# A two-layer graph attention network on one core: graph 0's means written over the gathered sums, graph 14's row made by TensorE, a root moved behind two sums on GpSimd

## The chip, the cores and the metric

The kernel runs on one NeuronCore of a Trainium2 chip. A core has five engines with a queue each: TensorE (PE in the profile, with PEld for its weight loads), VectorE (DVE), ScalarE (ACT), GpSimd (POOL) and SyncE (SP), which here issues DMAs alone. Each works off its queue in order and waits on semaphores of the others. The metric is the device time of one execution in microseconds (us); lower is better. The time before is the median of three runs.

## The reference

x holds 16 graphs of 1024 nodes with 256 features; adj is one 1024 x 1024 mask, the same for all graphs. All is in float32. Cut to what matters:

```python
def _gat(inp, adj_mask, W, a):             # layer 0, slope 0.2; h is normed, then relu
    h = inp @ W
    f1, f2 = h @ a[:F, 0], h @ a[F:, 0]
    e = leaky_relu(f1[:, :, None] + f2[:, None, :], ALPHA)
    if adj_mask is not None:
        e = where(adj_mask > 0, e, NEG_INF)
    return elu(softmax(e, axis=2) @ h)

# layer 0
h = maximum(layernorm(x), 0)
res = relu(h @ mlp1_w + mlp1_b)                         # 256 -> 512
out = elu(_gat(res, None, W_fc, a_fc)) + res            # dense attention, 512
res = relu(out @ mlp2_w + mlp2_b)                       # 512 -> 256
out = elu(_gat(res, adj, W_hand, a_hand)) + res         # masked attention
x = x + relu(out)
# layer 1
h = maximum(layernorm(x), 0)
x = x + relu(softmax(masked leaky_relu scores, slope 0.01) @ (h @ W))
```

## The kernel before, in words

Nodes are tiled by 128 (NT = 8 tiles, two halves of TH = 4). Every graph b goes through these stages:

- first norm (`Norm`, norm1): statistics of each tile on VectorE (L262, L263), the root 1/sqrt(var + eps) of a half on GpSimd (`root`, L267 and L268), centring on VectorE (`center`, L272), transposes on TensorE (`turn`, L282) and their eviction on ScalarE (L286);
- `mlp1` (L456, L459) into resT, `Dense.project` (L470, evicted at L472, the query column moved by GpSimd at L474 and L475) into h_nat;
- the dense attention without its 1024 x 1024 products: rows are ranked by their score (`rank`, VectorE), scattered to DRAM in that order by GpSimd's indirect DMAs (`scatter`, L530), read back by SP (`read_sorted`, L574), summed from both ends (`sum_before`, `sum_behind`, L602 to L617), the running sums written as a fine table (L609) and a coarse one (`carry`, L621 to L631). `sign` (ScalarE, L553) counts for each node where its own score falls, `count` turns the counts into indices, and `gather` (GpSimd, L642) fetches for each node the fine sums and adds the coarse ones to them in `got`. `share` (L654 to L657) gives the denominators, `mean` (L664 on ScalarE, L666 on VectorE) the weighted means `hp`;
- `merge` transposes hp on TensorE (L713), takes the lower part (L715), two exponentials on ScalarE (L716, L717); `merge_end` adds on VectorE (L723) and GpSimd adds into resT (L724); `mlp2` follows (L731, L734);
- masked attention `Gnn0` ("a"): `project` (L322, L324), `vectors`, `row` (the query weights as a row on all partitions), `scale` (L369), `weight` (VectorE, L375), `product` (L385), `finish`, `combine` with the sums on GpSimd (L413, L414) and `update` of x on VectorE (L418);
- second norm (norm2), then masked attention `Gnn1` ("b") and the store.

`row` exists in two ways. For b in AHEAD (1 to 14) `send` transposes the column on TensorE (L243), copies it on ScalarE (L245), writes it to DRAM (L246), and `row(True)` reads it back to all partitions by a DMA on SP (L360). For the others eight transposes on TensorE write it to PSUM (L238), and ScalarE copies it in two pieces (L365).

Graph 0 is an exception (`split`): its first half of the dense attention is done by real products (`Dense.weight` L687, `Dense.product` L695, `product_mean` L702 to L706, into tiles hpd of the same tag `hp`), its second half by gathers as above.

The order of everything is written by hand. `at(lo, hi, steps)` puts steps into a table with due times in us; the table is sorted by these times and the steps are issued in that order (L1091), which is the order in each engine's queue. The times mean nothing else. GpSimd's instructions, too, are chained in this order. The stages of neighbouring graphs overlap; a graph comes every PERIOD = 142. For graph b's masked attention t0 is its base and lo = t0 + 18 for b in AHEAD.

Tiles come from pools by tag with a number of buffers: `hp` has 4, `part` 2, `e2` 3, `hm` 2, `att` 8; in PSUM `mm` 4, `tr` 2, `bc` 1. A tile waits until the earlier user of its buffer is read out.

The lines that the change touches, besides those in its diff: `first_norm` places norm1's statistics and roots; `masked_first` places `send`, `row`, `scale`, `weight`, `product`, `finish`, `combine`, `update`, `stats` and the two roots of norm2; the schedule of the opening is written out from START = -168. `early_gathers` places a middle graph's sixteen gathers: four fine ones at t0 + 41.5 and 42.5, four from t0 + 48.5, the coarse ones from t0 + 53.5.

Of the kernel before, what the change touches and what calls it, by code (L numbers as in the profile page):

```python
# [8 lines left out]
F32 = mybir.dt.float32  # L9
# [8 lines left out]
P = 128  # L18
# [13 lines left out]
def fast_path(ctx: ExitStack, tc: tile.TileContext, alarm, x, adj, w1, b1, w2, b2, w_fc, a_fc,  # L32
# [24 lines left out]
    NT = N // P  # L57
# [3 lines left out]
    TH = HALF // P  # L61
    R = H + 2
    K = H + 1
# [3 lines left out]
    work = ctx.enter_context(tc.tile_pool(name="work", bufs=2))  # L67
# [154 lines left out]
    def at(lo, hi, steps):  # L222
        for i, step in enumerate(steps):
            table.append((lo + (hi - lo) * i / len(steps), len(table), step))
# [212 lines left out]
    class Dense:  # L437
# [221 lines left out]
        def mean(self, h, u):  # L659
            n = TH // len(self.got[h])  # L660
            got, den = self.got[h][u // n][:, u % n, :], self.dens[h]
            name = f"{self.b}_{h}_{u}"
            part = work.tile([P, K], F32, tag="part", name=f"part_{name}")
            nc.scalar.activation(part, got[:, :K], AF.Copy, scale=den[:, 1, u:u + 1])  # L664
            hp = self.hps[h, u] = work.tile([P, K], F32, tag="hp", name=f"hp_{name}", bufs=TH)
            nc.vector.scalar_tensor_tensor(hp, got[:, K:], den[:, 0, u:u + 1], part,  # L666
                                           op0=OP.mult, op1=OP.add)

# [104 lines left out]
    def each(f, *ranges):  # L773
        out = [()]
        for r in ranges:
            out = [o + (i,) for o in out for i in r]
        return [partial(f, *o) for o in out]

    def first_norm(t0, b):

        n = norm1[b]
        lo = t0 - (62 if b == 2 else 33.5)
        at(lo, lo + 1, n.stats_steps(0))
        at(t0 - 13, t0 - 9, n.stats_steps(1))
        n.turn_at(t0 - (14.5 if b == 2 else 22), 0, 4 if b == 2 else 7)
        n.turn_at(t0 + 0.2, 1, 4)
# [49 lines left out]
    def gathers(d, h, lo, hi):  # L836
        at(lo, lo + 4, each(d.gather, [h], [0], range(TH)))
        at(hi, hi + 7, each(d.gather, [h], [1], range(TH)))
# [20 lines left out]
    def merges(lo, d, h):  # L859
        at(lo, lo + 9.2, each(d.merge, [h], range(HC)))  # L860
        at(lo + 2.5, lo + 11.7, each(d.merge_end, [h], range(HC)))

    def second_mlp(t0, b, after=0):
        d, m = dense[b], gnn0[b]
        for i, lo in enumerate((102.5, 104.8, 113, 116.5)):
            lo += t0 - 3.4 * last(b)
            at(lo, lo, [partial(d.mlp2, i // FC, i % FC)])
        t0 += after
        at(t0 + 135, t0 + 142, each(m.project, range(NT)))
        at(t0 + 141.9, t0 + 141.9, [m.extremes])  # L870

    def weights(m, t, n, lo, hi):
        at(lo, hi, each(m.weight, [t], [n], range(NT)))

    def masked_first(t0, b):
        m, n = gnn0[b], norm2[b]
        at(t0 + 1, t0 + 1, [m.vectors])
        lo = t0 + 11
        if b in AHEAD:
            at(t0 + 3.4, t0 + 3.4, [m.send])  # L880
            at(t0 + 6, t0 + 6, [partial(m.row, True)])
            lo += 7
        else:
            at(t0 + 4, t0 + 4, [m.row])
        at(t0 + 4.5, lo - 1, each(m.scale, range(NT)))
        weights(m, 0, 2, lo - 5.5, lo - 1)
        at(t0 + 10, t0 + 10, [partial(load_again, b)])
        if last(b, 2):
            for q, start in enumerate((0.5, 2, 4.2, 5.5)):
                at(t0 + start, t0 + start, [partial(dense[b].natural, q)])  # L890
        else:
            at(t0 + 4.5, t0 + 11, each(dense[b].natural, range(NT // 2)))
        pairs = [(t, 2) for t in range(0, NT, 2)]
        if last(b):
            pairs[-1:] = [(NT - 2, 1), (NT - 1, 1)]
        for t, n_t in pairs:
            start = lo + 3.5 * t
            at(start, start + 3.5 * n_t, each(m.product, [t], [n_t], range(NT)))
            if t:
                weights(m, t, n_t, start - 5.5, start + 1)  # L900
        for t in range(NT):
            end = lo + 7.2 + 7 * (t // 2) + 0.6 * (t % 2)
            if last(b) and t == NT - 2:
                end -= 3.5
            at(end, end, [partial(m.finish, t)])
            at(end + 1.2, end + 1.2, [lambda t=t: m.combine(t, dense[b].o_nat)])
            if last(b) and t >= NT - 2:
                at(end + 2.6, end + 2.6, [lambda t=t: m.add(t, dense[b].o_nat, nc.vector)])
                end -= 2
            at(end + 5.2, end + 5.2, [lambda t=t: m.update(t, xs[b])])  # L910
            end += 5.6 if last(b) else 6.2 if b == 0 else 9
            at(end, end, [partial(n.stats, t)])
        at(lo + 25 - 3.4 * last(b), lo + 25 - 3.4 * last(b), [partial(n.root, 0)])
        lo += 33.1 if last(b) else 35.5 if b == 0 else 38.5
        at(lo, lo, [partial(n.root, 1)])

    def last(b, n=1):
        return b >= NB - n
# [58 lines left out]
    AHEAD = range(1, NB - 1)  # L977
# [4 lines left out]
    START = -168.0  # L982
    n, d = norm1[0], dense[0]
# [7 lines left out]
    n = norm1[1]  # L991
# [26 lines left out]
    for t in range(TH):  # L1018
        lo = START + 95 + 7.1 * t
        at(lo, lo + 7, each(d.product, [t], range(NT)))  # L1020
        at(lo + 8.2, lo + 8.2, [partial(d.product_mean, t)])
    at(START + 100, START + 107, each(d.weight, [1], range(NT)))
    gathers(d, 1, START + 108, START + 114)
    e = dense[1]
    at(START + 95.5, START + 95.5, [e.columns])
    at(START + 98.5, START + 98.5, [e.row, e.highest])
    at(START + 99, START + 118, each(e.rank, range(NT)))
    at(START + 118, START + 118, [less_columns])
    merges(START + 125, d, 0)
    at(START + 135, START + 135, [partial(d.share, 1)])  # L1030
    at(START + 135.5, START + 137, each(d.mean, [1], range(TH)))
    merges(START + 138.2, d, 1)
    second_mlp(START + 39, 0, -13)
    at(START + 123.4, START + 141, each(e.project, range(NT), [0]))
    scatters(e, START + 126, START + 142)
# [1 line left out]
    at(START + 142.5, START + 142.5, [e.read_sorted])  # L1037
    at(START + 76, START + 76, [partial(load_first, 2)])
    first_norm(0, 2)
    at(START + 147, START + 147, [e.sums_begin])  # L1040
    at(START + 144, START + 158, each(e.sign, range(NT)))
    for h in range(2):
        at(START + 150 + 3 * h, START + 150 + 3 * h, [partial(e.sums_weights, h)])
        at(START + 151 + 5 * h, START + 156 + 5 * h, each(e.sum_before, tiles(h)))
# [6 lines left out]
    for b in range(NB):  # L1051
        base, after_base = base_of(b), base_of(b + 1)
        masked_first(base, b)
        second_norm(base, b)
        pairs = range(0, NT, 2)
# [25 lines left out]
        if b + 3 < NB:  # L1081
            lo = after_base - PERIOD + 86
            at(lo, lo, [partial(load_first, b + 3)])
            first_norm(after_base, b + 3)
# [5 lines left out]
    with tc.manual_schedule(engines={engine.PE, engine.DVE, engine.Activation, engine.SP}):  # L1090
        for _, _, step in sorted(table, key=lambda entry: entry[:2]):  # L1091
            traced = nc.cur_bb.bb.instructions
            n = len(traced)
# [424 lines left out]
def two_layer_gat(tc, *args):  # L1518
    nc = tc.nc
    with tc.tile_pool(name="alarm", bufs=1) as pool:  # L1520
        alarm = pool.tile([1, 1], I32, name="alarm")
        fast_path(tc, alarm, *args)
        with tc.If(nc.values_load(alarm[0:1, 0:1], min_val=0, max_val=1,
                                  skip_runtime_bounds_check_because="it is 0 or 1") > 0):
            general_path(tc, *args)
# [24 lines left out]
```

## Time and profile before

| what | us |
|---|---|
| three runs | 2348.07, 2344.05, 2342.45 |
| median | 2344.05 |
| the profiled execution, its own time | 2359.75 |
| its span, first to last instruction | 2357.9 |
| idle before GpSimd's norm roots (L267), until VectorE's statistics | 148.4 in 35 waits |
| VectorE idle before the update of x (L418), until GpSimd's sum | 55.5 in 14 waits |
| GpSimd idle before a fine gather, until the fine table landed | 41.9 in 7 waits |

The span is the time between the first and the last instruction in the profile; the profiled execution is some 16 us longer than the median of the runs. Idle time of an engine costs only where the engine that bounds the kernel waits for it. In a timeline line the columns are start, duration, engine, line, operation, output<-inputs, shape and count; the bracket gives the idle time before it and what ended that. Neighbouring records of one line are merged. [...]

### The profile page before, as it was taken

The page shows a single profiled execution, that of the slowest core. Times are in us where ns is not written, and L with a number is a line of the kernel's source. Part 1 is how long each engine was busy: PE and PEld are TensorE (multiplying, and loading weights), DVE is VectorE, ACT ScalarE, POOL GpSimd, SP SyncE. Part 2 cuts the span into 40 slices and gives each one's busy share as a digit, 9 for nine tenths or more (in the row PEclk, how much of TensorE's full clock was granted, in tenths as well). Part 3 has the DMA queues.
Part 4 walks back from the last instruction along what each step waited for, and adds up shares of the span by engine and source line. Part 5 has one row for each costly group of instructions (what it writes and reads, how often), then busy time and mean ns, then how long its engine had stood idle before and what let it go on. Part 6 is the DMA issues. An engine that isn't in the chain of part 4 may idle for free. (4 is left out here: it accounts for less than half of the span.)

```text
span 2357.9 us, 30868 instructions
## 1 busy us (share of the span) xinstructions
PE 2268.6 (96%) x9955; PEld 1747.4 (74%) x9955; DVE 1625.7 (69%) x4535; ACT 1241.3 (53%) x2744; POOL 951.4 (40%) x1212
## 2 busy tenths in 40 slices
PE   8989999999999999999999999999999999999888
PEld 6667787777878778786776877777786876877666
DVE  6666685866858567685866867576685856767655
ACT  5345655647365463745546374554736546373442
POOL 1153435354443536334263543526444353533420
PEclk9999999999999999999999999999999999999999
DMA  4658366572656747366573745657265673737500
GB/s 173 165 159 210 72 176 165 167 193 97 200 118 175 180 143 184 97 187 161 172 187 113 186 115 165 174 161 181 91 195 143 174 184 125 185 95 182 140 21 27
DMA packets 150874, 355.81 MB, mean 151 GB/s; under 512 B 11224, under 2 KB 62760, under 8 KB 146608
## 3 DMA queue, kind: packets, MB, share of 16 engines
q1 hardware_dynamic: 104080, 189.58, 28.8%
q0 software_dynamic: 45952, 163.99, 26.3%
q8 instruction: 82, 1.34, 0.2%
q14 instruction: 88, 0.72, 0.1%
q10 hardware_dynamic: 672, 0.17, 0.0%
HBM read 227.40 MB, written 126.30 MB: 150 GB/s over the span
## 5 line engine op out<-in xcount | busy, mean ns | idle before, releaser
L385 PE MATMUL ob<-hmb,attb 128*128 128x257 f32 x2048 | 467.9, 386 | 21.4 <-DVE attb L375 17.0
L470 PE MATMUL h<-wfc_sb,resT 128*128 128x257 f32 x2048 | 465.7, 380 | 0.0
L385 PE MATMUL oa<-hma,atta 128*128 128x258 f32 x2048 | 454.7, 381 | 7.2 <-DVE atta L375 7.1
L385 PEld LDWEIGHTS ob<-hmb,attb 128*128 128x128 f32 x2048 | 387.2, 192 | 88.1 <-DVE attb L375 21.0
L385 PEld LDWEIGHTS oa<-hma,atta 128*128 128x128 f32 x2048 | 387.6, 190 | 67.0 <-issue 5.1
L470 PEld LDWEIGHTS h<-wfc_sb,resT 128*128 128x128 f32 x2048 | 379.5, 190 | 53.5 <-issue 0.7
L724 POOL TENSOR_TENSOR resT<-resT,e 128x512 f32<-128x512 f32 x128 | 163.6, 1278 | 371.4 <-DVE e L723 330.1
L375 DVE SCALAR_TENSOR_TENSOR atta<-rowsa,qwda,edge 128x256 f32<-128x256 f32 (+1 forms) x520 | 268.4, 545 | 27.6 <-PE oa L385 12.8
L413 POOL TENSOR_TENSOR posa<-posa,onat 128x256 f32<-128x256 f32 x118 | 98.7, 836 | 461.8 <-ACT posa L401 461.6
L375 DVE SCALAR_TENSOR_TENSOR attb<-rowsb,qwdb,edge 128x256 f32<-128x256 f32 (+1 forms) x536 | 247.9, 503 | 8.9 <-PE ob L385 5.5
L427 ACT ACTIVATE rb<-ob,recb 128x256 f32<-128x256 f32 x128 | 59.0, 475 | 346.1 <-DVE recb L425 329.4
L456 PE MATMUL m<-hT,w_sb 128*128 128x512 f32 x512 | 235.0, 598 | 0.5 <-ACT posa L401 0.5
L731 PE MATMUL m<-resT,w_sb 128*128 128x512 f32 x512 | 230.3, 596 | 4.3 <-POOL resT L724 4.3
L642 POOL DMA_INDIRECT got<-coarse,k x124 | 200.7, 1618 | 38.9 <-issue 37.7
L400 ACT ACTIVATE ea<-oa,reca 128x256 f32<-128x256 f32 x128 | 60.7, 474 | 271.2 <-DVE reca L397 262.1
L715 DVE TENSOR_SCALAR e<-hpT 128x512 f32<-128x512 f32 x128 | 88.3, 690 | 134.3 <-PE hpT L713 101.4
L731 PEld LDWEIGHTS m<-resT,w_sb 128*128 128x128 f32 x512 | 93.9, 191 | 106.3 <-issue 90.9
L456 PEld LDWEIGHTS m<-hT,w_sb 128*128 128x128 f32 x512 | 92.6, 193 | 95.9 <-issue 91.7
L642 POOL DMA_INDIRECT got<-fine,k x124 | 125.7, 1013 | 74.4 <-DMA fine<-xs 41.9
L530 POOL DMA_INDIRECT sorted<-hnat,place x128 | 131.9, 1030 | 39.6 <-issue 20.5
L553 ACT ACTIVATE junk<-r,fs 128x1024 int8<-128x1024 f32 x124 | 142.4, 1149 | 8.7 <-POOL fs L474 5.3
L716 ACT ACTIVATE e<-e 128x512 f32<-128x512 f32 x128 | 80.7, 631 | 84.2 <-DVE e L715 84.1
(186 smaller groups left out, 3445.8 us busy)
## 6 DMA issues: line engine op xcount, KB each, us to landing
xs<-sorted SPq DMA_DIRECT2D x32, 1028.0 KB
fine<-tt SPq DMA_DIRECT2D x32, 1026.0 KB
fine<-xs SPq DMA_DIRECT2D x32, 1026.0 KB
x<-in_x_dram SPq DMA_DIRECT2D x16, 1024.0 KB
xn<-in_x_dram SPq DMA_DIRECT2D x15, 1024.0 KB
out_dram<-x SPq DMA_DIRECT2D x28, 512.0 KB
coarse<-carry SPq DMA_DIRECT2D x32, 256.5 KB
r<-row_r SPq DMA_DIRECT2D x14, 512.0 KB
```

Source lines behind the costliest of these rows:

```text
L375: nc.vector.scalar_tensor_tensor(a_t[:, :n * P], self.rows[:, i], self.qwd[:, 1, j:j + 1], edge[:, j, i], op0=OP.max, op1=OP.mult)
L385: nc.tensor.matmul(self.out[t][:, :F + self.ONES], lhsT=self.att[t0, j][:, (t - t0) * P:(t - t0 + 1) * P], rhs=self.hm[:, j, 2:2 + F + sel ...
L413: adder.tensor_add(pos, pos, o_nat[:, t, :])
L456: nc.tensor.matmul(ps, lhsT=w1_sb[:, kc, c * P:(c + 1) * P], rhs=hT[:, kc, h * HALF:(h + 1) * HALF], start=(kc == 0), stop=(kc == FC - 1))
L470: nc.tensor.matmul(ps[:, :F + 1], lhsT=self.resT[:, kc, t * P:(t + 1) * P], rhs=wfc_sb[:, kc, g, :], start=(kc == 0), stop=(kc == HC - 1))
L530: made = nc.gpsimd.indirect_dma_start(out=sorted_d[self.b % 2], out_offset=bass.IndirectOffsetOnAxis(ap=self.place[:, t:t + 1], axis=0), i ...
L553: nc.scalar.activation(junk, self.r2, AF.Sign, bias=self.fs[:, 0, t:t + 1], accum_out=self.signs[:, t:t + 1])
L642: nc.gpsimd.indirect_dma_start(out=got[u // n][:, u % n, :], out_offset=None, in_=(coarse_d if coarse else fine_d)[self.b % 2][:, :], in_o ...
L715: nc.vector.tensor_scalar_min(e, ps, 0.0)
L716: nc.scalar.activation(e, e, AF.Exp)
L724: nc.gpsimd.tensor_add(dst, dst, e)
L731: nc.tensor.matmul(ps, lhsT=w2_sb[:, kc, c * P:(c + 1) * P], rhs=self.resT[:, kc, h * HALF:(h + 1) * HALF], start=(kc == 0), stop=(kc == H ...
```

## The change

Five things change.

1. `mean` writes graph 0's hp over the half of the gathered tile that it has just read, instead of into a tile of the tag `hp`.
2. The opening: the first half of graph 2's first statistics and root comes at due time -49 instead of -62; graph 0's gathers come 7 to 8 earlier; `product_mean` 0.6 earlier; `share`, `mean` and the merges of its second half 5, 5 and 2.2 earlier; graph 1's `sign` steps 14 to 8 earlier.
3. Graph 14's row in `Gnn0` is made by `row()` on TensorE and ScalarE, and no longer by `send` and `row(True)`. The later steps keep their places (lo is still t0 + 18).
4. The root of norm2's first half comes at lo + 31.5 instead of lo + 25 for graphs 1 to 14. On GpSimd it was between the fourth fine gather and the sums of tiles 6 and 7; it is now behind these sums and the fifth gather.
5. Graph 0 and the last graph keep their place for this root (lo + 25 and lo + 21.6).

```diff
             part = work.tile([P, K], F32, tag="part", name=f"part_{name}")
             nc.scalar.activation(part, got[:, :K], AF.Copy, scale=den[:, 1, u:u + 1])
-            hp = self.hps[h, u] = work.tile([P, K], F32, tag="hp", name=f"hp_{name}", bufs=TH)
+            hp = self.hps[h, u] = got[:, K:] if self.split else work.tile(
+                [P, K], F32, tag="hp", name=f"hp_{name}", bufs=TH)
             nc.vector.scalar_tensor_tensor(hp, got[:, K:], den[:, 0, u:u + 1], part,
                                            op0=OP.mult, op1=OP.add)
...
     def first_norm(t0, b):
         n = norm1[b]
-        lo = t0 - (62 if b == 2 else 33.5)
+        lo = t0 - (49 if b == 2 else 33.5)
         at(lo, lo + 1, n.stats_steps(0))
...
         lo = t0 + 11
         if b in AHEAD:
+            lo += 7
+        if b in AHEAD and not last(b, 2):
             at(t0 + 3.4, t0 + 3.4, [m.send])
             at(t0 + 6, t0 + 6, [partial(m.row, True)])
-            lo += 7
         else:
             at(t0 + 4, t0 + 4, [m.row])
...
-        at(lo + 25 - 3.4 * last(b), lo + 25 - 3.4 * last(b), [partial(n.root, 0)])
+        root = lo + (21.6 if last(b) else 25 if b == 0 else 31.5)
+        at(root, root, [partial(n.root, 0)])
...
         at(lo, lo + 7, each(d.product, [t], range(NT)))
-        at(lo + 8.2, lo + 8.2, [partial(d.product_mean, t)])
+        at(lo + 7.6, lo + 7.6, [partial(d.product_mean, t)])
     at(START + 100, START + 107, each(d.weight, [1], range(NT)))
-    gathers(d, 1, START + 108, START + 114)
+    gathers(d, 1, START + 101, START + 106)
...
     merges(START + 125, d, 0)
-    at(START + 135, START + 135, [partial(d.share, 1)])
-    at(START + 135.5, START + 137, each(d.mean, [1], range(TH)))
-    merges(START + 138.2, d, 1)
+    at(START + 130, START + 130, [partial(d.share, 1)])
+    at(START + 130.5, START + 135, each(d.mean, [1], range(TH)))
+    merges(START + 136, d, 1)
     second_mlp(START + 39, 0, -13)
     at(START + 123.4, START + 141, each(e.project, range(NT), [0]))
...
-    at(START + 144, START + 158, each(e.sign, range(NT)))
+    at(START + 130, START + 150, each(e.sign, range(NT)))
```

## The prediction

> **What bounds the kernel now.** I read the busy shares and the slices first, then the timeline of TensorE for each place that the diff names, then the other engines there.
>
> ```profile
> PE 2268.6 (96%) x9955; PEld 1747.4 (74%) x9955; DVE 1625.7 (69%) x4535; ACT 1241.3 (53%) x2744; POOL 951.4 (40%) x1212
> PE   8989999999999999999999999999999999999888
> ```
>
> TensorE (PE) is busy 96% of the span, so only its idle time can be won. The change adds and removes almost no matmuls (one transpose goes, eight come). Idle time lies in the first graphs and in the last, some 1 us a graph between. First place, graph 0's second merge (TensorE, except the third line, GpSimd's root of graph 2's first norm):
>
> ```profile
> 143.07 5.37 PE L470 MATMUL h<-wfc_sb,resT 128*128 128x257 f32 x24
> 152.65 0.33 PE L713 MATMUL hpT<-ident,hp 128*128 128x128 f32 x1 [1.73 <-DVE hp L666]
> 122.24 0.23 POOL L267 TENSOR_SCALAR rstd<-mv 128x4 f32<-128x4 f32 x1 [48.03 <-DVE mv L263]
> 124.80 2.01 PE L695 MATMUL od<-hnat,attd 128*128 128x257 f32 x8 [1.55 <-ACT hpd L705]
> 153.58 3.28 PE L470 MATMUL h<-wfc_sb,resT 128*128 128x257 f32 x8
> 167.91 1.13 PE L731 MATMUL m<-resT,w_sb 128*128 128x512 f32 x2 [1.14 <-POOL resT L724]
> 169.95 2.03 PE L731 MATMUL m<-resT,w_sb 128*128 128x512 f32 x2 [0.92 <-POOL resT L724]
> 176.90 7.14 PE L322 MATMUL pa<-wh_sb,oT 128*128 128x258 f32 x32
> ```
>
> PE runs out of projections at 148.4, waits for the means hp until 153.3, and later twice for the sums resT. GpSimd sat 48 us in front of a root; the gathers of graph 0 queue behind it and end near 137.
>
> Second place, a middle graph (GpSimd, VectorE, TensorE):
>
> ```profile
> 631.52 1.04 POOL L642 DMA_INDIRECT got<-fine,k  x1 [0.30 <-issue]
> 632.92 1.04 POOL L268 TENSOR_TENSOR rstd<-rstd,power 128x4 f32<-128x4 f32 x1
> 633.96 0.72 POOL L413 TENSOR_TENSOR posa<-posa,onat 128x256 f32<-128x256 f32 x1
> 635.51 0.93 DVE L418 SCALAR_TENSOR_TENSOR x<-ea,x 128x256 f32<-128x256 f32 x1 [2.97 <-POOL ea L414]
> 637.19 1.08 POOL L642 DMA_INDIRECT got<-fine,k  x1 [0.16 <-issue]
> 645.56 0.83 POOL L267 TENSOR_SCALAR rstd<-mv 128x4 f32<-128x4 f32 x1
> 648.32 1.43 PE L282 MATMUL nt<-ident,hn 128*128 128x128 f32 x8 [0.42 <-DVE hn L272]
> 780.27 4.55 PE L385 MATMUL ob<-hmb,attb 128*128 128x257 f32 x12 [3.55 <-DVE attb L375]
> ```
>
> VectorE waits 2.97 us for tile 6's sum, because GpSimd does four gathers and the root first. In this graph PE doesn't feel it; its one wait is for the second half's root. One graph later, where a table landed late, it does (3.55).
>
> Third place, graph 14:
>
> ```profile
> 2131.80 0.32 SPq L360 DMA_DIRECT2D rowsa<-row_a  x1
> 2136.31 0.48 DVE L375 SCALAR_TENSOR_TENSOR atta<-rowsa,qwda,edge 128x256 f32<-128x256 f32 x1 [3.02 <-DMA rowsa<-row_a]
> 2136.94 5.43 PE L385 MATMUL oa<-hma,atta 128*128 128x258 f32 x23 [2.44 <-DVE atta L375]
> ```
>
> The row's broadcast lands 4.5 us after its issue, and PE stands 2.44 us for it.
>
> [...] after the gap at 148.4 eight records take 3.28 us where 1.90 is usual. [...] the update at 635.51 takes 0.93 beside a GpSimd sum, 0.41 without one. [...] Here a row's way out and back is dearer: written at 2127.02, read issued at 2131.80, used at 2136.31.
>
> **Part 1, graph 0 and the opening: -4.9 us.** The eight gathers go ahead of the root. The tables they read are issued by 108.6 and eight gathers took 13.2 us (123.79 to 136.98), so they end some 10 us before their use at about 141. The four sums of statistics (0.54 us each, 2.2) leave the ranks on VectorE and come after them; so the mean of row tile 1 (VectorE 124.02) comes at 121.9, and the 1.55 wait goes: everything after is 1.55 earlier. The statistics then run 129.3 to 131.4 and meet nobody. The first merge's transposes end at 141.5.
> The share now follows the first merge's second sum, on VectorE at 140.8. On ScalarE the eight sign sums (1.27 each with their read-out) now stand between the steps of the merges; none is hidden by an idle queue here. In the order of the new due times: hnat copy to 141.8, sign to 143.2, two parts (0.65 each) to 144.5; VectorE's two means to 145.3, the held-back e(0,3) to 145.9; ScalarE's two exponentials 147.2, copy 147.5, sign 148.8, two parts 150.1; VectorE's last mean 150.85. It was 153.26. Writing into the gathered tile removes the wait for the first merge's four hp tiles, which otherwise would end at 141.5 anyway: worth nothing by itself. PE, having done h_5 at 145.0, transposes at 151.0, with h_6 and h_7 still ahead where only h_7 was: 153.58 against 151.0 + 1.74, a gain of 0.84. Then it runs beside ScalarE: h_6 at half clock to 154.1, hpT, h_7 to 156.3, hpT, m to 160.2, hpT, m to 164.1. ScalarE: copy 154.4, sign 155.6, e(1,1) 156.9, copy, sign 158.5, e(1,2) 159.8, bias 160.9, sign 162.3, e(1,3) 163.6. VectorE 164.3, GpSimd's sum 165.7 (was 169.9). The next m needs it at 166.7: the waits of 1.14 and 0.92 and the half clock after them go. Transposes 167.6 to 168.4, m to 171.9, and pa starts there, not at 176.90: 5.0 earlier. The following transposes need hn, which goes through xs, landing about 8.6 us after an issue near 161 (so long the second half took at 2124.93): 179.0 against 183.88, so 4.9. Graph 1's scatters move with the projections; its chain keeps its distance. Ends: -8 if the first gap keeps full clock and ScalarE is ahead[...].
>
> **Part 2, graph 14's row: -3.1 us.** Gone: one transpose, a copy (0.24), two DMAs, and on SP a wait in front of graph 14's x load and the first table write. New: eight transposes (0.87 on PE, as at 188.30) and two copies (1.07 on ScalarE, as at 189.37), in front of the o_nat copies; PE's ob products cover them but for some 0.25. ob then ends at 2134.75; the first weight follows the four sums before it on VectorE (end 2133.3) and is ready at 2133.8. So oa starts at 2134.75 instead of 2136.94: 2.2. Later in this graph GpSimd waited 3.67 for a table to land, then PE 3.43. With 0.5 MB less and SP free 6 us sooner that may shrink by 0 to 3.7; I take 0.9, since the queues thin out (DMA share 0.5) before it lands. Ends -1.5 and -6.
>
> **Part 3, the root in 14 graphs: +0.8 us.** The root (1.37 with its start) leaves the front of four sums and goes behind one gather. The sum of tile 6 ends 1.37 earlier, the update and two weights too. Then hn, next on VectorE, waits: sums end 635.66, gather to 636.9, root 1.40 to 1.63 (the later is the cost after a gather at 644.54), so hn at about 638.4; it was 638.04. VectorE trades a wait of 2.97 for 1.6 and 1.7. The third weight comes 0.3 to 0.5 later, and PE waits for it already (0.32 in most graphs). But the second root stands behind the same GpSimd work and isn't moved; PE's wait there (0.42 plus some 0.4 in its transposes) takes the delay up. Only graphs without that wait pay, two in this trace: 2 x 0.4. Ends: -7 (case C) and +15 (case D). The later root queues nothing else but three gathers, 1.4 later at the most.
>
> Sum: -4.9 - 3.1 + 0.8 = -7.2 us. The profiled execution took 2359.75 (span 2357.9), so 2352.5; the runs shown are 15.7 faster at the median, 2344.05, and I take the same difference: 2336.9.
>
> **Rivals.** A, this forecast: 0.46.
> B, ScalarE becomes the bound of the opening: six sign sums, 7.6 us, stand in front of the last exponential, and [...]GpSimd's last sum comes at 169 as before. For: ScalarE has more to do there than PE (about 20 us against 16). Against: the sum came out 4 us early. Left: about -2.2 from the row, 2342. 0.20.
> C, the update's gain reaches PE. For: six graphs show waits of 3.55, 3.43, 2.47, 1.61, 1.01 and 0.53 for the weight after tile 6's update; 1.37 less of each is 7.0. Against: the third weight ends last. 2329. 0.20.
> D, slower: the root behind the gather holds VectorE. With the gap of 0.31 after a gather and the root's longest durations (0.85 and 1.28) hn comes 1.1 us later, and if the second root slips as well, 14 x 1.1 = 15.4: 2351.5. It decides from 8.0 / 14 = 0.57 a graph. Against: the second root has the same work in front. 0.14.
>
> **How the numbers follow.** About 0.3% (7 us) is what a measurement can tell from no change. A lies on that edge: 0.26 of its 0.46 is faster, 0.20 same. B is same, C faster, D 0.12 slower and 0.02 same. Faster 0.46, same 0.42, slower 0.12. The range 2329 to 2348 leaves out D and the far half of C.
>
> **What would show it.** The gathers of graph 0 ahead of the root, the means' end near 151, pa near 172 and no wait for resT; in graph 14 oa without a wait for rowsa; in middle graphs tile 6's update waiting about 1.6, hn about 1.7, the transposes of the second half where they were. Wrong if pa starts after 175, or if the middle graphs' period changes by more than 0.5 us either way.

## The result, and the profile after

| | before | after |
|---|---|---|
| median of 20 runs, us | 2348.01 | 2352.30 |
| lowest to highest | 2340.48 to 2350.78 | 2346.50 to 2356.58 |
| ratio, 95% interval | | 1.0017 [1.0009, 1.0025] |
| profiled execution, its own time (span) | 2359.75 (2357.9) | 2353.19 (2351.5) |

The change makes the kernel slower by 0.17%, some 4 us; the forecast was 7.2 us faster. The two profiles say the opposite, 6.4 us less span. The profile of before is the odd one: its execution is 9 us above the slowest of the 20 timed runs. A second profile of before, taken later, has a span of 2350.0 us.

The first fence is TensorE's timeline in graph 0's second merge after the change, the second the same of graph 14. The change adds a line, so L666, L713 and L731 of before are L667, L714 and L732 here.

```profile
141.83 3.63 PE L470 MATMUL h<-wfc_sb,resT 128*128 128x257 f32 x16
150.77 0.44 PE L714 MATMUL hpT<-ident,got 128*128 128x128 f32 x1 [3.16 <-DVE got L667]
151.70 3.17 PE L470 MATMUL h<-wfc_sb,resT 128*128 128x257 f32 x8
161.19 7.03 PE L732 MATMUL m<-resT,w_sb 128*128 128x512 f32 x16
172.37 7.14 PE L322 MATMUL pa<-wh_sb,oT 128*128 128x258 f32 x32
```

```profile
2124.97 1.09 PE L238 MATMUL rowspsa<-ident,qwda 128*128 128x128 f32 x8 [0.37 <-ACT qwda L347]
2133.71 14.08 PE L385 MATMUL oa<-hma,atta 128*128 128x258 f32 x64
```

Both places are as forecast: the last mean is there at about 151, no line waits for resT, pa starts at 172.37 (176.90 before), and graph 14's oa follows without a wait for its row.

So the loss is to be looked for in the middle graphs. Here is the graph shown in the prediction, in the timelines of GpSimd, VectorE and TensorE after the change:

```profile
635.46 0.96 POOL L642 DMA_INDIRECT got<-fine,k  x1 [0.15 <-issue]
636.45 0.25 POOL L267 TENSOR_SCALAR rstd<-mv 128x4 f32<-128x4 f32 x1
638.02 1.21 POOL L642 DMA_INDIRECT got<-fine,k  x1 [0.19 <-issue]
639.53 1.33 POOL L642 DMA_INDIRECT got<-fine,k  x1 [0.31 <-issue]
641.17 0.94 POOL L642 DMA_INDIRECT got<-fine,k  x1 [0.30 <-issue]
645.37 0.86 POOL L267 TENSOR_SCALAR rstd<-mv 128x4 f32<-128x4 f32 x1
633.78 0.94 DVE L418 SCALAR_TENSOR_TENSOR x<-ea,x 128x256 f32<-128x256 f32 x1 [0.62 <-POOL ea L414]
637.86 0.73 DVE L272 TENSOR_SCALAR hn<-x,mv,rstd 128x256 f32<-128x256 f32 x2 [1.47 <-POOL rstd L268]
660.84 0.16 DVE L654 TENSOR_TENSOR den<-got,qd 128x4 f32<-128x4 f32 x1 [3.61 <-DMA got<-coarse,k]
648.16 1.41 PE L282 MATMUL nt<-ident,hn 128*128 128x128 f32 x8 [0.42 <-DVE hn L272]
663.88 0.33 PE L714 MATMUL hpT<-ident,hp 128*128 128x128 f32 x1 [0.24 <-DVE hp L667]
664.77 0.33 PE L714 MATMUL hpT<-ident,hp 128*128 128x128 f32 x1 [0.56 <-DVE hp L667]
665.43 0.33 PE L714 MATMUL hpT<-ident,hp 128*128 128x128 f32 x1 [0.33 <-DVE hp L667]
665.60 1.90 PE L470 MATMUL h<-wfc_sb,resT 128*128 128x257 f32 x8
```

And the lines of before, VectorE and TensorE, to which the forecast gave no place:

```profile
660.13 0.16 DVE L654 TENSOR_TENSOR den<-got,qd 128x4 f32<-128x4 f32 x1 [2.72 <-DMA got<-coarse,k]
664.71 0.33 PE L713 MATMUL hpT<-ident,hp 128*128 128x128 f32 x1 [0.34 <-DVE hp L666]
664.88 1.90 PE L470 MATMUL h<-wfc_sb,resT 128*128 128x257 f32 x8
```

The update's wait fell to 0.62, where 1.6 was forecast, and hn waits 1.47 (forecast 1.7). PE is at the second half's transposes (nt) 0.16 us earlier than before, yet at the projection behind the means (h, L470) 0.72 later. Between them PE waits for the means hp. These wait for VectorE's denominators (den), and those for the landing of the first half's coarse gathers.

To compare executions, times below are counted from a graph's first fine gather and averaged over 11 middle graphs (2 to 12). There the period, from one graph's first gather to the next's, is 140.44 us after the change and 138.93 with the root put back. Each is one execution: four more, whose middle graphs are those of before (before twice, the opening alone, the row alone), have periods of 139.08 to 140.55, so a period can be off by 1 us. The denominators are steadier: at 33.3 us after the change, at 32.3 to 32.6 in these four and with the root put back.

### The profile page after: what moved, and what is told of

It is laid out like the page before. It is cut to its first block, busy times and chain, and to the rows that moved or that the text cites. A ratio compares the mean times of both kernels' runs of the same rounds, so it can differ in the third digit from the quotient of the medians.

```text
span 2351.5 us, 30884 instructions
## 1 busy us (share of the span) xinstructions
PE 2266.0 (96%) x9962; PEld 1746.3 (74%) x9962; DVE 1639.0 (70%) x4535; ACT 1241.4 (53%) x2745; POOL 955.1 (41%) x1212
## 5 line engine op out<-in xcount | busy, mean ns | idle before, releaser
L385 PE MATMUL ob<-hmb,attb 128*128 128x257 f32 x2048 | 461.1, 382 | 18.7 <-DVE attb L375 14.8
L470 PE MATMUL h<-wfc_sb,resT 128*128 128x257 f32 x2048 | 465.7, 380 | 0.0
L470 PEld LDWEIGHTS h<-wfc_sb,resT 128*128 128x128 f32 x2048 | 379.4, 190 | 53.5 <-issue 0.7
L375 DVE SCALAR_TENSOR_TENSOR attb<-rowsb,qwdb,edge 128x256 f32<-128x256 f32 (+1 forms) x536 | 259.1, 525 | 8.9 <-PE ob L385 5.5
L732 PE MATMUL m<-resT,w_sb 128*128 128x512 f32 x512 | 229.6, 596 | 2.2 <-POOL resT L725 2.2
L732 PEld LDWEIGHTS m<-resT,w_sb 128*128 128x128 f32 x512 | 94.2, 192 | 104.6 <-issue 92.2
L530 POOL DMA_INDIRECT sorted<-hnat,place x128 | 132.2, 1033 | 39.6 <-issue 20.6
```

The source lines that it names most:

```text
L375: nc.vector.scalar_tensor_tensor(a_t[:, :n * P], self.rows[:, i], self.qwd[:, 1, j:j + 1], edge[:, j, i], op0=OP.max, op1=OP.mult)
L385: nc.tensor.matmul(self.out[t][:, :F + self.ONES], lhsT=self.att[t0, j][:, (t - t0) * P:(t - t0 + 1) * P], rhs=self.hm[:, j, 2:2 + F + sel ...
L470: nc.tensor.matmul(ps[:, :F + 1], lhsT=self.resT[:, kc, t * P:(t + 1) * P], rhs=wfc_sb[:, kc, g, :], start=(kc == 0), stop=(kc == HC - 1))
L530: made = nc.gpsimd.indirect_dma_start(out=sorted_d[self.b % 2], out_offset=bass.IndirectOffsetOnAxis(ap=self.place[:, t:t + 1], axis=0), i ...
L732: nc.tensor.matmul(ps, lhsT=w2_sb[:, kc, c * P:(c + 1) * P], rhs=self.resT[:, kc, h * HALF:(h + 1) * HALF], start=(kc == 0), stop=(kc == H ...
```

## The experiments

Each ratio is to runs of the kernel before taken next to those of the experiment. The medians of before in the four groups of experiments ran from 2341.5 to 2349.1 us, so only ratios are compared. What the profiles say of a kernel comes from one execution of it.

### One part at a time

Three theories. T1: the moved root costs its 0.8 us a graph or more and hides what the other parts gain. T2: the root is free, and the gains of the opening and of the row are lost later. T3: late tables alone, in some executions.

The root put back, all else as changed:

```diff
-        root = lo + (21.6 if last(b) else 25 if b == 0 else 31.5)
-        at(root, root, [partial(n.root, 0)])
+        at(lo + 25 - 3.4 * last(b), lo + 25 - 3.4 * last(b), [partial(n.root, 0)])
```

> The changed kernel with the root of the second norm's first half back at its old place (lo + 25), all else as changed. Theory T1, the moved root costs some 0.8 us in each of 14 graphs and hides what the other parts bring: this kernel is 6 to 9 us faster than the kernel before (ratio 0.996 to 0.9975), some 11 faster than the changed one; first fine gather to second root about 17.8 us again instead of 18.1. Theory T2, the opening's and the row's gains are lost further on and the root costs what the prediction said, 0.8 us in all: within 2 us of the changed kernel, ratio 1.001 to 1.003. Theory T3, the difference is how often a table lands late, whatever the root's place: ratio 0.999 to 1.003 with late landings as many as in the changed kernel.

The root alone moved, all else as before:

```diff
-        at(lo + 25 - 3.4 * last(b), lo + 25 - 3.4 * last(b), [partial(n.root, 0)])
+        root = lo + (21.6 if last(b) else 25 if b == 0 else 31.5)
+        at(root, root, [partial(n.root, 0)])
```

> The kernel before with the root alone moved to lo + 31.5. T1: 8 to 12 us slower than before, ratio 1.0035 to 1.005, the third weight after tile 6's update later in each graph and first gather to second root 0.27 us longer. T2: at most 1 us slower, ratio 1.000 to 1.0005. T3: anything from 1.000 to 1.003, by the late landings.

Only the opening with graph 0's means (the change's hunks for `mean`, `first_norm` and START):

```diff
-    gathers(d, 1, START + 108, START + 114)
+    gathers(d, 1, START + 101, START + 106)
...
-    at(START + 144, START + 158, each(e.sign, range(NT)))
+    at(START + 130, START + 150, each(e.sign, range(NT)))
```

> The kernel before with the opening alone (means over the gathered sums, gathers, merges, signs and graph 2's statistics at their new times); row and root as before. T1: graph 0's masked projection starts near 172.4 as in the changed kernel and the 4.5 us stay to the end, ratio 0.9975 to 0.9985. T2: the start is as early, but the end isn't, ratio 0.9995 to 1.002.

Only graph 14's row:

```diff
         if b in AHEAD:
+            lo += 7
+        if b in AHEAD and not last(b, 2):
```

> The kernel before with graph 14's row alone made by TensorE. T1 and T2 differ little here: the wait for the row goes (2.2 us), and what a late table costs in graph 14 may go too: ratio 0.997 to 0.9992. If the row's place doesn't matter since graph 14 waits for its table anyway, 0.9995 to 1.0005.

| run | ratio, 95% interval | worked out, us |
|---|---|---|
| root put back | 0.9966 [0.9954, 0.9978] | -8.0 |
| root alone | 1.0075 [1.0061, 1.0088] | +17.6 |
| opening alone | 0.9983 [0.9976, 0.9991] | -4.0 |
| row alone | 0.9988 [0.9979, 0.9997] | -2.8 |

The microseconds are the ratio less 1, times before's 2341.5. The opening and the row bring about what the forecast gave them, -4.9 and -3.1, and their sum is close to the gain with the root put back. The root loses 17.6 us alone, and 1.0017 / 0.9966 = 1.0051 or 12 us on top of the rest. T2 and T3 fall. T1 has the place, but for the root alone its range ended at 1.005: the loss is larger than it said.

### What of the moved root costs

T4: its place between the fifth and the sixth gather makes the later gathers land late. T5: VectorE is held, as hn waits for the root and the weights stand behind hn.

The changed kernel with the root in front of the fifth gather, still behind the sums:

```diff
-        root = lo + (21.6 if last(b) else 25 if b == 0 else 31.5)
+        root = lo + (21.6 if last(b) else 25 if b == 0 else 30.25)
```

> The whole change, but the first half's root comes directly behind the four sums of tiles 6 and 7 and in front of the fifth gather (in the changed kernel it is behind that gather). T4, the gathers: what costs is that the root now stands between the fifth and the sixth fine gather; in the traces so far the sixth to eighth start 0.3 us later, and the first half's coarse gathers land 1.0 us later (33.3 against 32.3 us after the first fine gather). With the root in front of the fifth gather these starts are as with the old place, the landing is back at 32.3, PE's wait for the means falls from 0.9 to about 0.4 us a graph, and the time is that of the kernel with the root put back: 0.9966 of before, 0.9955 to 0.9980. T5, VectorE: what costs is that hn waits for the root behind the sums, and the weights behind hn; the root still comes 3.1 us later than in the old place, so at least half of the cost stays: 0.999 to 1.001.

The root put back, and an addition of no use on GpSimd in front of the sixth gather:

```diff
+        def pause(self):
+            spare = small.tile([P, TH], F32, tag="spare", name=f"spare{self.name}")
+            nc.gpsimd.tensor_scalar_add(spare, self.mv[:, :TH, 1], EPS)
...
+        if b in AHEAD:
+            at(lo + 31.5, lo + 31.5, [n.pause])
```

> The change with the root put back in its old place, and in graphs 1 to 14 one small extra addition on GpSimd (128x4, some 0.3 us with its start, its result unused) between the fifth and the sixth fine gather. T4: 0.3 us there is the cost by itself: the landing of the first half's coarse gathers moves from 32.3 to about 33 us after the first gather, PE's wait for the means grows by 0.3 to 0.6 us a graph, 5 to 14 us in all: 0.999 to 1.002 of before. T5: VectorE isn't touched, so only the second root moves, by 0.3 us x 14 = 4 us at the most: 0.9966 to 0.9983.

The changed kernel, and then the kernel with the root put back, each with the load of a later x taken from among the gathers:

```diff
...
-            lo = after_base - PERIOD + 86
-            at(lo, lo, [partial(load_first, b + 3)])
+            lo = after_base - PERIOD + 94
+            at(lo, lo, [partial(load_first, b + 3, nc.scalar)])
```

> The whole change, and the load of the x of the graph after the next two (1 MB) is issued by ScalarE's queue behind the means, some 20 us later than SP issues it now (24.7 us after the first fine gather, in the middle of the coarse gathers); its first use is at 64 us. T4: the gathers land earlier without that megabyte among them[...]; PE's wait for the means (0.9 us a graph) is gone, and only the second root's 0.3 us stays: 0.9966 to 0.9985 of before. T5: PE's waits for the means are a by-product of its being late and VectorE is as before: 1.0005 to 1.002.

> The change with the root in its old place, and the same late load of x. T4: PE's wait for the means, 0.4 us a graph, goes: 5 us less than the kernel with the root put back, 0.9945 of before (0.993 to 0.9955). T5: nothing but a by-product, 0.9966 (0.996 to 0.9975).

Measured: 1.0055 [1.0035, 1.0076], 0.9983 [0.9973, 0.9993], 1.0015 [1.0005, 1.0025] and 0.9964 [0.9950, 0.9978]. Neither theory had the first number. With the root in front of the fifth gather, GpSimd and TensorE in the graph shown above:

```profile
635.48 1.07 POOL L268 TENSOR_TENSOR rstd<-rstd,power 128x4 f32<-128x4 f32 x1
636.75 1.21 POOL L642 DMA_INDIRECT got<-fine,k  x1 [0.19 <-issue]
638.26 1.33 POOL L642 DMA_INDIRECT got<-fine,k  x1 [0.31 <-issue]
639.90 0.94 POOL L642 DMA_INDIRECT got<-fine,k  x1 [0.31 <-issue]
647.92 1.41 PE L282 MATMUL nt<-ident,hn 128*128 128x128 f32 x8 [1.20 <-DVE hn L272]
```

A gather's issue takes 0.94 us at its quickest, but the two that follow this root take 1.21 and 1.33; after the change too it is the two behind the root, the sixth and seventh. The root sets VectorE's centring (hn) free. The first of the two issues runs beside it for most of its time (1.06 us on average after the change); the second meets only its last 0.17 us, and then other work of VectorE. In the old place the sixth issue has 0.69 us of centring beside it and takes 1.00, the seventh has none and takes 1.12. So these issues are longer in the new order, but what makes them so isn't shown. All four gathers go out late here (the last ends at 15.2 after the first gather, 14.6 with the old place); the second root starts 0.6 later, PE waits 1.20 for the transposes, and the denominators come at 33.9. Against T5, hn came earlier than in the old place (9.65 against 10.34), and PE's waits for the weights are few (1.6 us in the table below), and still the kernel is slower. T4 had wrongly assumed that equal work takes GpSimd equal time.

The pause leaves VectorE and the second root alone (17.85 against 17.83), moves the denominators from 32.3 to 32.8, and costs 4 us against the kernel with the root put back; the two intervals just overlap. It speaks for the landing, since T5's reason, a later second root, isn't there, but it doesn't decide: the ratio is below T4's range and at the upper end of T5's. The pause was no clean dose either: the seventh gather's issue became shorter by 0.15.

The late load changed nothing that can be told: both ratios lie in T5's ranges, and the fourth coarse gather lands at 33.1 as in the changed kernel. T4 was wrong to name this megabyte as what the gathers compete with.

### The landing, or the second root

T6: a graph pays for the landing of the fourth coarse gather. T7: it pays for the second root, for which PE waits 0.42.

The root of the first half in its old place, the second root one coarse gather earlier:

```diff
-        at(t0 + 53.5, t0 + 68, coarse)
+        at(t0 + 54.5, t0 + 68, coarse)
...
-        lo += 33.1 if last(b) else 35.5 if b == 0 else 38.5
+        lo += 33.1 if last(b) else 35.5 if b == 0 else 38.1
```

> The change with the first half's root in its old place, and in graphs 1 to 13 the root of the second half one coarse gather earlier on GpSimd (behind the first coarse gather instead of the second). T6, the landing: a graph's period follows the moment when the fourth coarse gather has landed (VectorE's denominators at 32.3, 32.8, 33.3 and 33.9 us after the first fine gather went with periods of 138.9, 139.7, 140.4 and 141.3). The second root, 1.9 us earlier, ends PE's wait of 0.42 us for the second half's transposes, but the wait for the means takes the same amount on; no gain: 0.996 to 0.9975 of before. T7, the second root: PE's wait for these transposes is what a graph pays, and 0.42 x 13 = 5.5 us go: 0.9943 (0.993 to 0.9955).

The first root behind all eight fine gathers, with the centring and transposes that need it moved:

```diff
+        root = lo + (21.6 if last(b) else 25 if b == 0 or last(b, 2) else 35.2)
+        at(root, root, [partial(n.root, 0)])
...
-            n.turn_at(t0 + 60.3, 0, 7)
+            n.turn_at(t0 + 64.3, 0, 4.2)
             n.turn_at(t0 + 67.3, 1)
```

> As the kernel with the root put back, but in graphs 1 to 13 the first half's root stands behind all eight fine gathers, and what needs it (the centring on VectorE, the transposes on PE) is moved behind the weights and some 3 us later in the products, so that neither engine has to wait for it. T6: the fifth to the eighth fine gather go out 1.4 us earlier than with the old place; the fourth coarse gather lands about 1 us earlier (31.3), PE's wait for the means goes (0.4 us a graph), 5 us in all: 0.9945 of before (0.993 to 0.9962). T7: the second root keeps its time, so no gain: 0.9966 (0.996 to 0.9985).

Both:

> The two moves of the last two runs together. T6 and T7 both: the landing is earlier and the second root too; PE loses the waits for the second half's transposes and for the means, 0.8 us a graph, 10 us in all: 0.992 of before (0.990 to 0.994). If it is no better than either alone, a further bound stands behind them (the next graph's tables).

Measured: 0.9986 [0.9979, 0.9993], 0.9927 [0.9914, 0.9940] and 1.0064 [1.0044, 1.0084]. The first ends PE's wait for the transposes and is slower than the kernel with the root put back: the second coarse gather goes out 1.3 us later, the denominators slip by 0.3, and PE, there earlier, waits 1.2 us for the means instead of 0.4. T7 falls, and T6 had not seen the later landing. The second is the fastest kernel of all, faster than both the kernel before and the changed one, and by more than T6 gave it (9 us against the root put back, not 5). PE hardly waits for the means; it waits more for the transposes' hn (12.3 us in the table below), and gains all the same. Its GpSimd, VectorE and TensorE:

```profile
628.47 0.96 POOL L642 DMA_INDIRECT got<-fine,k  x1 [0.15 <-PE ob L385]
632.22 0.94 POOL L642 DMA_INDIRECT got<-fine,k  x1 [0.31 <-issue]
633.19 0.36 POOL L267 TENSOR_SCALAR rstd<-mv 128x4 f32<-128x4 f32 x1
651.78 0.16 DVE L654 TENSOR_TENSOR den<-got,qd 128x4 f32<-128x4 f32 x1 [2.09 <-DMA got<-coarse,k]
655.82 0.87 PE L714 MATMUL hpT<-ident,hp 128*128 128x128 f32 x4
656.53 1.90 PE L470 MATMUL h<-wfc_sb,resT 128*128 128x257 f32 x8
```

The eighth gather goes out 11.9 us after the first (620.29), not 13.9 as after the change, and the last four issues take 0.94 to 0.96.

With both roots moved, the expected gain became the worst loss. TensorE:

```profile
659.14 0.33 PE L714 MATMUL hpT<-ident,hp 128*128 128x128 f32 x1 [0.27 <-DVE hp L667]
660.02 0.33 PE L714 MATMUL hpT<-ident,hp 128*128 128x128 f32 x1 [0.56 <-DVE hp L667]
660.69 0.34 PE L714 MATMUL hpT<-ident,hp 128*128 128x128 f32 x1 [0.34 <-DVE hp L667]
660.86 3.58 PE L470 MATMUL h<-wfc_sb,resT 128*128 128x257 f32 x8
```

PE comes earlier and the denominators come at 32.8 all the same, so it waits some 2.2 us a graph for the means. In 7 of 13 graphs the eight records of the projection behind that wait take 3.2 to 3.6 us instead of 1.90: there the wait is followed by 1.3 to 1.7 us of longer projection. In the graph of the fence the granted clock was 0.53 from 661.0 to 664.5. The size of the wait doesn't decide it: here it is 1.17 in three pieces, while another graph with 2.44 keeps 1.90.

### What makes the landing late

T9: the store of a finished graph, among the gathers, takes their place. T10: landings follow the issue alone. For the last winner also T8: the new order on PE and VectorE gained, not the gathers.

The root in its old place, only the centring and the transposes moved (the `turn_at` line above):

> A control to the kernel with the root behind the gathers: the root of the first half is in its old place, and only the centring on VectorE and the transposes on PE are moved, exactly as there. T6, the landing: the gathers go out when they did with the old place, the fourth coarse gather lands at 32.3 us after the first fine gather, and there is no gain: 0.9966 of before (0.9955 to 0.998). T8, the order on PE and VectorE is what gained (no wait of the third weight): 0.9927 (0.9914 to 0.994).

The changed kernel, and then the kernel with both roots moved, each with one late store by ScalarE's queue in place of two by SP:

```diff
...
+            elif t + n == NT and not last(b, 3):
+                late = base_of(b + 1) + 94
+                at(late, late, [lambda: m.store(0, NT, xs[b], b, nc.scalar)])
-            elif t % TH + n == TH:
+            elif t % TH + n == TH and last(b, 3):
                 at(end + 2.8, end + 2.8, [lambda t=t: m.store(t // TH * TH, TH, xs[b], b)])
```

> The whole change, and the two stores of a finished graph (512 KB each, issued by SP at 14 and 24 us after the first fine gather, among the gathers) become one of 1 MB, issued by ScalarE's queue some 48 us after it, for graphs 0 to 12. T9, the store collides: the late gathers lose their place to the store; without it the eighth fine gather lands by 20.5 us instead of 22.3, the fourth coarse by 31 instead of 33.2, PE's wait for the means (0.9 us a graph) goes: 0.995 to 0.998 of before. T10, the issue alone: landings follow the moment at which GpSimd issues the gathers, whatever else moves: as the changed kernel, 1.0017 (1.0005 to 1.0025).

> The kernel with both roots moved, and the same late store. T9: the coarse gathers land 1.5 to 2 us earlier (31.0 instead of 32.8), PE keeps neither the wait for the means nor that for the second half's transposes: 0.992 of before or less (0.988 to 0.994). T10: as with both roots moved, 1.0064 (1.004 to 1.0085).

The kernel before, once more:

> The kernel before, unchanged, for a second profile of it. If the profile of before was of an unusually long execution, this one's span is about 2345 us instead of 2357.9, with fewer gathers of GpSimd waiting for a table.

Measured: 0.9943 [0.9930, 0.9956], 0.9971 [0.9959, 0.9983] and 0.9939 [0.9921, 0.9956]; the second profile of before has a span of 2350.0 us (about 2345 was expected), with GpSimd waiting for a fine table in two of graphs 1 to 13 instead of five.

The late store takes the changed kernel from 1.0017 to 0.9971 and the one with both roots from 1.0064 to 0.9939, with no gather issued earlier by more than 0.1 us. Each of the next fences shows one instruction alone, the eighth fine gather of the graph shown above: first with the change, then with the late store.

```profile
L642 POOL DMA_INDIRECT got<-fine,k x1: 938/938/938, 641.2 to 641.2; - x1
DMA to landing us min/median/max: 8.7/8.7/8.7
```

```profile
L642 POOL DMA_INDIRECT got<-fine,k x1: 941/941/941, 638.7 to 638.7; - x1
DMA to landing us min/median/max: 6.5/6.5/6.5
```

Issued 13.9 us after the first gather in both, it takes 8.7 us to land in one and 6.5 in the other. With the root put back it was 7.6. T10 falls, and T9 has the ratios and the eighth gather right. Two of its details missed: the denominators came at 32.0 in the changed kernel, where it had the fourth coarse gather by 31, and with both roots moved PE still waits 12.8 us for the means.

The moved centring alone gives 0.9943, between the kernel with the root put back (0.9966) and the one with the root behind the gathers (0.9927), and its interval touches both. T6 and T8 may each have a share in that gain; how much isn't settled.

Together, from the traces: the landing is averaged over six middle graphs, the denominators over eleven, and PE's waits are summed from 330 to 2050 us, for the means (hp), for the transposes' hn and for the weights attb of the second masked attention. A dash stands where the trace doesn't show it.

| kernel | eighth fine gather landed | denominators | waits for hp, us | for hn | for attb | ratio |
|---|---|---|---|---|---|---|
| root behind gathers | 19.6 | 31.3 | 1.4 | 12.3 | 1.7 | 0.9927 |
| both roots, late store | - | 31.2 | 12.8 | 0 | 3.8 | 0.9939 |
| centring moved alone | - | 32.3 | 3.1 | 12.8 | 3.4 | 0.9943 |
| root put back | 21.3 | 32.3 | 5.1 | 5.7 | 2.8 | 0.9966 |
| changed, late store | 20.1 | 32.0 | 0.9 | 5.4 | 18.0 | 0.9971 |
| pause | 21.6 | 32.8 | 8.7 | 5.8 | 6.5 | 0.9983 |
| second root early | 21.6 | 32.6 | 14.3 | 0.8 | 6.9 | 0.9986 |
| changed | 22.3 | 33.3 | 11.1 | 5.0 | 12.2 | 1.0017 |
| root before fifth gather | 22.8 | 33.9 | 14.4 | 17.5 | 1.6 | 1.0055 |
| both roots | 19.7 | 32.8 | 27.1 | 0.5 | 0.9 | 1.0064 |

From the denominators to the first projection behind the means it is 4.75 to 4.87 us in every kernel of the table: wherever PE waits for hp, its place in the graph is set by this landing. The wait for hp alone doesn't order the kernels, and after the change PE's largest wait is another, for the weights, 12.2 us against 2.8 with the root put back: hn stands in front of the third weight. Behind it PE still waits for hn (5.0) and then for hp, so while the gathers land late, a shorter wait for the weights would only lengthen those. That is argued from the order of the waits; the kernel with the root before the fifth gather, with 1.6 us for the weights, is slower and fits it. With the late store the wait for hp is gone, and the one for the weights, 18.0, is what is left of T5.

## Why the prediction was wrong

- **Part 1, graph 0: right.** Its moments came within a microsecond: last mean about 151 (forecast 150.85), pa at 172.37 (171.9), no wait for resT. Measured alone it gave -4.0, forecast -4.9.
- **Part 2, graph 14's row: right.** -2.8 against -3.1. The row's two DMAs of before are issued by ScalarE and SP, with 4.8 us from the write's issue to the read's and 4.5 from there to the use, beside other transfers.
- **Part 3, the root: the step that failed.** The forecast's sum for it was +0.8 us; the runs show +12 to +17.6. Two sentences failed. "But the second root stands behind the same GpSimd work and isn't moved": it came 0.27 later in the median graph, since the issues of the sixth and seventh gather took 1.21 and 1.33 us there, against 1.00 and 1.12 in the old place. And "The later root queues nothing else but three gathers, 1.4 later at the most" counted these gathers at nothing. The start of the eighth was only 0.3 late, but the denominators came 0.7 to 1.0 us later, at a place where PE already waited 0.34 in this very graph of the profile of before. The forecast had read that PE's "one wait is for the second half's root" there, and some 1 us of idle time a graph; that profile has 26.4 us of waits from 330 to 2050, 2.2 a graph, 6.3 of them for the means. VectorE's new wait, on which the forecast spent its words, was sized about rightly for hn (1.47 against 1.7). PE's wait for the weights behind it grew by more than forecast, but stands in front of the waits for hn and the means.
- **Rival D had the part and the size** (1.1 us a graph, 15.4 in all), **not the carrier**, so its number is right by luck. It let hn come 1.1 late and the second root slip with it; hn came 0.26 later. The transposes of the second half are at 20.9 instead of 20.6; the denominators at 33.3 instead of 32.3. The argument against D, that the second root has the same work in front, took equal work for equal time.
- **Rival B** didn't come: the last sum of the opening started at 165.0, and no line of PE waits for it. **Rival C** didn't come either: tile 6's update was 1.3 us earlier in every graph, but the third weight 0.3 later, since hn stands in front of it.
- **From execution to median.** The forecast took 15.7 us from its profiled execution because the three runs shown were that much faster. That execution was an outlier, and the median of 20 runs of before is 2348.01, not 2344.05: the base was 4 us too low. Against this base -7.2 would have meant 2340.8, still far from 2352.3, so the root decides.

Open in part: why so small a delay at the issue becomes up to 1.0 us at the landing. The profile's sums over stretches go some way. The columns are the stretch, its length, PE's busy time with its records, the granted clock, the packets' own times as a share of the DMA engines' time (it can pass 1) and GB/s. First the changed kernel in the graph shown, 9 to 18 and 18 to 32 us after its first gather, then the same of the kernel with the root behind the gathers:

```profile
636.29:645.29 9.00, 8.41 (x43) 1.00 0.72 195
645.29:659.29 14.00, 13.58 (x59) 1.00 1.05 237
629.29:638.29 9.00, 9.00 (x46) 1.00 0.88 279
638.29:652.29 14.00, 13.80 (x61) 1.00 1.03 209
```

From 18 us to the landing the DMA engines have work all the time, as far as this share tells (1.05 and 1.03), so what wasn't moved before would land later. Over eleven graphs 3.77 MB are moved in the first 18 us after the change, 3.90 with the root put back, 4.59 with the root behind the gathers. At the 241 GB/s of the stretch that follows, the 0.13 MB missing after the change are worth an estimated 0.5 us; the rest is open. So is the store's share in the kernel with the root put back, where the late store wasn't tried. How a store by SP holds up GpSimd's gathers isn't shown either; measured is the 2.2 us between the two landings of the eighth.

## What to carry to other kernels

When an instruction moves on an engine that also issues DMAs, follow every transfer behind it to its landing, and to who waits for that landing now; ask whether a later wait takes the delay up. In the graph shown PE waited 0.34 us for the means before the change; after it the denominators came 0.71 us later and the projection behind the means 0.72. Look at whether the DMA engines are full further on: here their share was 0.72 in the 9 us from the moved root on and 1.05 in the 14 us behind these, and the eighth gather, issued 0.3 us later than with the root put back, landed 1.0 later on average (22.3 against 21.3). Look also at what the moved instruction sets free, since it will run beside what comes next: here the centring, beside a gather's issue of 1.21 us instead of 1.00. And take the base from many runs: here one profiled execution was 11.7 us above the median of runs that agree within 0.5%.

## What the runs showed of the hardware

- The issue of a gather (128 rows) on GpSimd takes 0.94 us at its quickest, and 1.21 and 1.33 for the two that follow the root in each kernel with the root behind the sums and next to a gather (medians of the middle graphs). The first of them runs beside VectorE's centring (128x256, SBUF to SBUF), the second mostly beside other work of VectorE. What makes the two longer isn't shown.
- Two stores of 512 KB on SP's queue, the first issued 14 us after the first gather, delay the landing of the eighth by 2.2 us: issued at 13.9 us in both, it lands after 8.7 us with them and after 6.5 without. As an estimate, 512 KB at the 241 GB/s measured from 18 to 32 us are 2.2 us too. A load of 1 MB on the same queue, issued at 24.7 us, didn't tell: with it some 20 us later the fourth coarse gather lands at 33.1 as in the changed kernel.
- Waits for the means of 1.2 to 3.0 us in a graph, broken by single transposes, were followed by the eight records of a projection in 3.2 to 3.6 us instead of 1.90 in 7 of 13 graphs of the kernel with both roots moved, and with waits of 1.4 and 1.6 us in two graphs of the one with the root before the fifth gather. In the changed kernel, with up to 1.2 us, no middle graph shows it. The sum of the waits doesn't tell the graphs apart.
- The forecast's "half clock" in graph 0 of before was a granted clock of 0.58 from 153.58 to 156.90, where eight records took 3.28 us, and of 0.51 from 170.0 to 172.0, behind the second wait for resT. After the change it was 0.60 from 151.70 to 154.87, with eight records in 3.17 us, and 1.00 from 166 to 172. At 1.00, from 154.87 to 158.0, eight records take 1.90.
- In the trace of before a float32 product has two records (L470: 1024 products, 2048 records) and a transpose one (L282: 512 and 512).
